# Counting pass of the routing graph's edge ranking: from layer 1's feed-forward to layer 0's, its table kept in DRAM in between

## The chip, the cores and the metric

The kernel is one program on one core of one Trainium2 chip. The metric is the device time of one execution in microseconds (us). Every time below is of this one core.

## What is computed

The reference is a graph transformer of four layers over 3125 nodes of 256 features. Each layer adds a message-passing step over 50,000 edges and a token mixer, then a feed-forward step. Cut to what this change touches:

```python
x = x + L0_gnn(xn, ...) + L0_mix(xn)
x = x + L0_ffn(layernorm(x))        # 8 experts of width 1024, one expert per node, capacity 489
xn = layernorm(x)
x = x + L1_gnn(xn, ...) + L1_mix(xn)
x = x + L1_ffn(layernorm(x))        # one router for all nodes: two of 8 experts, width 512, then a layer norm
...
x = x + L3_ffn(layernorm(x), L3_ffn_edge_index)   # a graph attention picks the experts
```

The last step has a graph of its own, `L3_ffn_edge_index`: 32,768 edges among 2048 nodes, in no order. Its attention is summed by destination node. The kernel therefore sorts these edges by destination long before layer 3: for each edge it computes its place in the sorted list. That depends on the input `L3_ffn_edge_index` alone, so it can be done at any time before the edges are moved, in layer 2's feed-forward.

## The kernel before, in words

The 3125 nodes are padded to 25 tiles of 128 nodes. The 32,768 routing edges stand in 256 chunks of 128 (one column of a 128 x 256 array each); a destination is split into its low seven bits (`ka`, the row in a tile) and its tile (`kt`, 0 to 15, `T2` = 16).

`route_places` (L2039) finds the places in three passes, and gives control back (`yield`) after each group of four chunks, so that a caller can mix it with other work:

- The counting pass. For each group, VectorE compares the low bits of 4 x 128 edges with a row of numbers (`within`, `r_oha`, L2073), and once in 32 chunks the tiles (`tiles`, `r_oht`, L2067). TensorE multiplies the two one-hot arrays, four bf16 products of 16 columns (`count`, L2081): how many edges of the chunk go to each node. ScalarE copies 32 chunks' counts into the table `r_by` (L2083).
- The scan. VectorE sums the table over all chunks (`deg2`, L2096), TensorE turns the sums into starting places (`starts`, L769 and L771), and for each of 16 tiles VectorE runs a prefix sum over the chunks and splits the result in two bytes, `hi` and `lo`, both kept in `r_by` (128 partitions x 2 x 16 x 256 values in bf16, that is 16 KB a partition, L2104 to L2109).
- The ranking pass. For each group, SyncE loads the edges' low bits as a row repeated on all partitions (`r_b`, from the DRAM array `rowa`, L2132); VectorE makes one comparison of it (`r_at`, L2135) and four masked ones (`r_m`, L2138); TensorE runs eight small products (`rank`, L2118 and L2119). After each 16 chunks VectorE picks the result (`r_sel`, `r_pos`, L2122 and L2125).

All three passes lie beside layer 1's feed-forward: `beside(self.l1_ffn(p, after1), (low, 3, 1))` in `fast` (L2621) takes three steps of `route_places` for each step of `l1_ffn` (L1542). Before its loop, `l1_ffn` computes the router from the mean of all nodes (`L1557` and the lines after it), and GpSimd gathers the two chosen experts' weights by index (L1582). Then it runs over seven blocks, six of four node tiles and one of a single tile: for each of two experts, matrix products into `hT` (L117 is the helper that issues them), ScalarE's Gelu, products back, and VectorE's additions into `z` (L1606). At the end of a block comes a layer norm on VectorE (L157 to L165, L1629 to L1631) and the next layer's norm and transposes (`after1`: `norm_tiles`, L182 to L193, transposes on TensorE L173), then the products for layer 2's table (`fill2`).

Layer 0's feed-forward, `l0_ffn` (L1186), runs alone before, as `for _ in self.l0_ffn(p, True, pr0)`. It computes each node's slot in its expert's list on VectorE (L1214 to L1231; `wi`, L1229, is the list of slots), GpSimd scatters 25 tiles of nodes into a DRAM buffer by those slots (`moe_buf`, L372), and for eight experts SyncE loads weights and slots (`xb`, L1248), TensorE transposes (L1253), one half of `xT` is copied by VectorE and one by ScalarE (L125 and L127), and the products run (L117), with VectorE adding the bias (`y`, L1265).

Beside both feed-forward steps a `Pump` releases one scatter of another sort (`by_src`, L372, on GpSimd) for every 700 columns of products in layer 0's step and every 560 in layer 1's; layer 2 starts with a load of the table that these fill.

The engines run their own instruction lists in order and wait for each other by semaphores. The order within each list is fixed when the program is built: GpSimd's is the order of the program text, the others' is set by a scheduler with a cost model of its own. So a generator that is placed beside another says how far ahead it may run, and the built program says in which order the instructions stand.

Of the kernel before, what the change touches and what calls it, by code (L numbers as in the profile page):

```python
# [7 lines left out]
F32 = mybir.dt.float32  # L8
# [75 lines left out]
def beside(main, *others):  # L84

    for i, _ in enumerate(main):
        for g, num, den in others:
            for _ in range((i + 1) * num // den - i * num // den):
                next(g, None)
# [11 lines left out]
class Net:  # L101
# [1934 lines left out]
                nc.scalar.copy(rec[:, :, k], self.load(tmp, n, a[n], dtype=I32))  # L2036
        return rec, place

    def route_places(self, pool, place):  # L2039

        nc = self.nc
        G = 4
        n, per = C2, 32
        dst = self.load(pool, "r_dst", self.a["dst2"], dtype=I32)
        ka = self.bits(pool, dst, "r_a", None, 127)  # L2050
        kt = self.bits(pool, dst, "r_t", 7)
        by = pool.tile([P, 2, T2, n], BF16, name="r_by")
        hi, lo = by[:, 0], by[:, 1]
        pos = pool.tile([P, n], F32, name="r_pos")
        rowa = self.dram.tile([1, n * P], BF16, name="rowa")
        rows_a = rowa.rearrange("o (c p) -> (o c) p", p=P)
        for c0 in range(0, n, P):
            p = self.ps(P)
            nc.tensor.transpose(p, ka[:, c0:c0 + P], self.ident)
            ra = pool.tile([P, P], BF16, name="r_ra", bufs=2)  # L2060
            nc.vector.tensor_copy(ra, p)
            nc.sync.dma_start(rows_a[c0:c0 + P], ra)
        ioa = self.iota2[:, None, :P].to_broadcast([P, G, P])

        def tiles(c0, w):
            oh = pool.tile([P, per, T2], BF16, name="r_oht", bufs=2)[:, :w]
            nc.vector.tensor_tensor(oh, self.iota2[:, None, :T2].to_broadcast([P, w, T2]),  # L2067
                                    kt[:, c0:c0 + w, None].to_broadcast([P, w, T2]), op=OP.is_equal)
            return oh

        def within(g):
            oh = pool.tile([P, G, P], BF16, name="r_oha", bufs=4)
            nc.vector.tensor_tensor(oh, ioa, ka[:, g * G:(g + 1) * G, None].to_broadcast([P, G, P]), op=OP.is_equal)  # L2073
            return oh

        late = []

        def count(g, oha, oht, p, c0):
            for j in range(G):
                k = g * G + j - c0  # L2080
                nc.tensor.matmul(p[:, k * T2:(k + 1) * T2], oha[:, j, :], oht[:, k, :], start=True, stop=True)  # L2081
            if (g + 1) * G == c0 + 32:
                nc.scalar.copy(lo[:, :, c0:c0 + 32], p.rearrange("p (c t) -> p t c", t=T2))  # L2083

        for c0 in range(0, n, per):
            oht = tiles(c0, per)
            p = self.ps(per * T2, name="acc")
            for g in range(c0 // G, (c0 + per) // G):
                late.append((g, within(g), oht, p, c0))
                if len(late) > 2:  # L2090
                    count(*late.pop(0))
                yield
        while late:
            count(*late.pop(0))
        nc.vector.memset(self.deg2, 0.0)
        nc.vector.tensor_reduce(self.deg2[:, :T2], lo, axis=AX.X, op=OP.add)  # L2096
        base = self.starts(pool, self.deg2[:, :T2], T2)
        one = pool.tile([P, n], BF16, name="r_one")
        nc.vector.memset(one, 1.0)
        for t in range(T2):  # L2100
            w = pool.tile([P, n], F32, name="r_w", bufs=2)
            wi = pool.tile([P, n], I32, name="r_wi", bufs=2)
            wl = pool.tile([P, n], I32, name="r_wl", bufs=2)
            nc.vector.memset(w[:, 0:1], 0.0)  # L2104
            nc.vector.tensor_tensor_scan(w[:, 1:], one[:, 1:], lo[:, t, :n - 1], 0.0, OP.mult, OP.add)
            nc.vector.tensor_scalar(wi, w, base[:, t:t + 1], None, op0=OP.add)
            nc.vector.tensor_scalar(wl, wi, 255, None, op0=OP.bitwise_and)
            nc.vector.tensor_copy(lo[:, t, :], wl)
            nc.vector.tensor_sub(hi[:, t, :], wi, wl)  # L2109
            yield  # L2110
        per //= 2

        def rank(g, at, m, oht, q, c0):
            for j in range(G):
                c = g * G + j
                k = c - c0
                v = q[:, k * 2 * T2:(k + 1) * 2 * T2]
                nc.tensor.matmul(v, at[:, j, :], by[:, :, :, c], start=True, stop=False)  # L2118
                nc.tensor.matmul(v[:, T2:], m[:, j, :], oht[:, k, :], start=False, stop=True)  # L2119
            if (g + 1) * G == c0 + per:  # L2120
                sel = pool.tile([P, per, 2 * T2], F32, name="r_sel", bufs=2)
                nc.vector.tensor_tensor(sel.rearrange("p c (b t) -> p c b t", b=2),  # L2122
                                        q.rearrange("p (c b t) -> p c b t", b=2, t=T2),
                                        oht[:, :, None, :].to_broadcast([P, per, 2, T2]), op=OP.mult)
                nc.vector.tensor_reduce(pos[:, c0:c0 + per], sel, axis=AX.X, op=OP.add)  # L2125

        for c0 in range(0, n, per):
            oht = tiles(c0, per)
            q = self.ps(per * 2 * T2, name="acc")
            for g in range(c0 // G, (c0 + per) // G):  # L2130
                b = pool.tile([P, G, P], BF16, name="r_b", bufs=4)
                nc.sync.dma_start(b.rearrange("p g e -> p (g e)"), bcast_rows(rowa[:, g * G * P:(g + 1) * G * P], G * P))  # L2132
                at = pool.tile([P, G, P], BF16, name="r_at", bufs=4)
                m = pool.tile([P, G, P], BF16, name="r_m", bufs=4)
                nc.vector.tensor_scalar(at, b, self.iop, None, op0=OP.is_equal)  # L2135
                for j in range(G):
                    c = g * G + j
                    nc.vector.scalar_tensor_tensor(m[:, j, :], b[:, j, :], ka[:, c:c + 1], self.triu16,  # L2138
                                                   op0=OP.is_equal, op1=OP.mult)
                late.append((g, at, m, oht, q, c0))  # L2140
                if len(late) > 2:
                    rank(*late.pop(0))
                yield
        while late:
            rank(*late.pop(0))
        self.rows_of(pool, pos, n, place)

        nc.vector.tensor_scalar(kt, kt, T2 - 0.5, 65536.0, op0=OP.is_gt, op1=OP.mult)
        nc.vector.tensor_add(place, place, kt)
        nc.vector.tensor_reduce(self.beyond, kt, axis=AX.X, op=OP.add)  # L2150
# [390 lines left out]
    def fast(self):  # L2541
# [3 lines left out]
        with tc.tile_pool(name="keepf", bufs=1) as keep, tc.tile_pool(name="dramf", bufs=1, space=DRAM) as dram:  # L2545
# [30 lines left out]
            with Banks(self, **plain):  # L2576
                sorted_e = dram.tile([P * C1, 3], F32, name="by_src")
                send = self.send(sorted_e, place, rec, C1)
                for _ in range(16):
                    next(send)  # L2580
                with tp("ffn0") as p:
                    self.pump = Pump(tc, send, 700)
                    for _ in self.l0_ffn(p, True, pr0):
                        pass


            with tp("att1") as gp:
# [17 lines left out]
            with Banks(self, **plain):  # L2605
                route = tp("route")
                rec4, place4 = self.route_lists(route.__enter__())
                by_dst = dram.tile([P * C2, 2], F32, name="by_dst")
                nc.sync.dma_start(by_dst.rearrange("(p c) f -> p (c f)", p=P).rearrange("p (k f) -> p k f", k=2),
                                  self.zeros[:, None, :].to_broadcast([P, 2, D]))  # L2610
                self.dlin2 = dram.tile([1, lin_size(C2)], F32, name="dlin2")
                send4 = self.send(by_dst, place4, rec4, C2)
                with tp("set2") as sp, tp("low") as lp, tp("ffn1") as p:
                    tab, fill2 = self.linear_table("tab2", sp, self.load(sp, "w", wtile(a["L2_gnn_W"])))

                    def after1(t0, n):
                        self.norm_tiles(t0, n)
                        fill2(t0, n)
                    self.pump = Pump(tc, send, 560)
                    low = self.route_places(lp, place4)  # L2620
                    beside(self.l1_ffn(p, after1), (low, 3, 1))  # L2621
                    self.pump = None
                    for _ in low:
                        pass
                for _ in send:
                    pass
# [322 lines left out]
```

## Time and profile before

| | |
|---|---|
| median of 3 runs | 4421.31 us (4421.1 to 4431.99) |
| profiled execution: its own time / its span | 4425.03 us / 4423.3 us |
| mean granted TensorE clock in it | 0.851 |
| TensorE products busy | 3472.8 us, 79% |
| VectorE busy | 2187.9 us, 49% |
| ScalarE busy | 913.9 us, 21% |
| GpSimd busy | 2620.9 us, 59% |
| layer 0's feed-forward, products of the experts | about 726 to 952 us |
| layer 1's feed-forward, from the router's product to the last table row | about 1679 to 2085 us |

In the profile's lines PE is TensorE's products, PEld its weight loads, DVE VectorE, ACT ScalarE, POOL GpSimd and SP SyncE. A line of the timeline gives start, duration, engine, line of the kernel, operation, output and inputs, their shapes and the number of instructions merged; the bracket at its end is the idle time of the engine just before, and what ended it. A line of the chain of waits gives start and length of one piece of the chain of work that ended last. A line of the table of windows gives, for each engine, its busy time in that stretch and the number of instructions, then the granted TensorE clock, the share of the DMA engines' time and the rate.

### The profile page before, as it was taken

The numbers are of one execution on the slowest core, as the hardware profiler recorded it, in microseconds if no ns is written. First come the engines' busy times: TensorE is split into PE (matmuls) and PEld (weight loads), VectorE is DVE, ScalarE is ACT, GpSimd is POOL, SyncE is SP. The second block draws the span as 40 slices with busy tenths as digits, with TensorE's granted clock in tenths as the row PEclk, the third lists the DMA queues.
The fourth block names the chain that finished last, engine by engine and source line by source line (L and its number), as shares of the span: only waits on it lengthen the run. The fifth ranks groups of instructions, "written<-read, shape, count | busy, mean of one in ns | idle before, by whom it ended". The sixth has DMA issues, their size and how long they took to land.

```text
span 4423.3 us, 45241 instructions
## 1 busy us (share of the span) xinstructions
PE 3472.8 (79%) x12927; PEld 2207.6 (50%) x12927; DVE 2187.9 (49%) x7489; ACT 913.9 (21%) x1841; POOL 2620.9 (59%) x2609
## 2 busy tenths in 40 slices
PE   8778875963866776686887758996969899669999
PEld 3446543642433443454555434553546577346666
DVE  4576531125777777676445452111255723354554
ACT  2110001210211112112311021221213233132433
POOL 0577776774777765664777734674027656617661
PEclk9888876986877876787988968997979999769999
DMA  3433333323533331022333320000023433421110
GB/s 142 154 98 98 101 97 121 112 59 97 158 101 96 106 92 44 10 51 56 109 106 121 119 88 1 14 10 13 29 74 108 129 93 98 127 61 15 20 15 13
DMA packets 231337, 349.00 MB, mean 79 GB/s; under 512 B 74144, under 2 KB 168151, under 8 KB 231080
## 3 DMA queue, kind: packets, MB, share of 16 engines
q0 software_dynamic: 108384, 219.50, 18.2%
q1 hardware_dynamic: 118280, 122.48, 8.9%
q10 hardware_dynamic: 4416, 4.01, 0.3%
q8 instruction: 110, 1.80, 0.2%
q14 instruction: 147, 1.20, 0.1%
HBM read 295.13 MB, written 50.61 MB: 78 GB/s over the span
## 4 chain that ended last, share of the span: by engine, by line
PE 59%; DVE 15%; DMA 13%; issue 7%; POOL 3%; ACT 2%; SPq 0%; POOLq 0%; DVEq 0%; ACTq 0%
PE mm L117 37%; PE seg L461 10%; DMA G<-tab,e3src 4%; PE seg L445 4%; DMA G<-h_tab,gi 3%; DMA ring<-l1rows,e1src 1%; DMA G<-tab,e1src 1%; PE mm L173 1%; DVE E L457 1%; POOL G L496 1%; DVE ring L912 1%; DVE ln_st L182 1%; DVE r_m L2138 1%; PE mm L1427 1%; PE ga L868 1%
## 5 line engine op out<-in xcount | busy, mean ns | idle before, releaser
L461 PE MATMUL seg<-G,E 128*128 128x257 f32 (+1 forms) x1564 | 503.9, 446 | 144.0 <-DMA G<-h_tab,gi 72.3
L117 PE MATMUL mm<-xnT,w 128*128 128x512 f32 (+1 forms) x1232 | 543.1, 580 | 4.8 <-DVE x L2319 4.5
L496 POOL DMA_INDIRECT G<-h_tab,gi x391 | 384.1, 982 | 257.3 <-DMA rb_L_gnn_self_b<-in_L_gnn_self_b 122.7
L372 POOL DMA_INDIRECT by_src<-rec,place x391 | 418.2, 1070 | 189.3 <-PE mm L117 123.2
L900 POOL DMA_INDIRECT ring<-l1rows,e1src x391 | 438.8, 1122 | 119.9 <-issue 63.1
L457 DVE TENSOR_SCALAR E<-iota_row,e1dl 128x128 f32<-128x128 f32 x1173 | 334.0, 299 | 321.0 <-PE seg L461 305.3
L496 POOL DMA_INDIRECT G<-tab,e1src x391 | 384.1, 982 | 182.5 <-PE seg L461 109.8
L461 PEld LDWEIGHTS seg<-G,E 128*128 128x128 f32 x1564 | 301.0, 213 | 328.5 <-DVE E L457 112.1
L496 POOL DMA_INDIRECT G<-tab,e3src x391 | 387.7, 992 | 123.4 <-PE seg L445 60.0
L461 PE MATMUL seg<-ring,E 128*128 128x264 f32 (+1 forms) x1294 | 366.7, 396 | 93.5 <-DVE E L457 66.0
L445 PE MATMUL seg<-G,E 128*128 128x256 f32 x1070 | 328.3, 433 | 112.8 <-DMA G<-tab,e3src 84.4
L117 PE MATMUL mm<-w,hT 128*128 128x256 f32 (+1 forms) x1712 | 415.0, 389 | 0.7 <-ACT hT L1619 0.5
L372 POOL DMA_INDIRECT by_dst<-rec,place x256 | 252.0, 984 | 193.9 <-PE mm L117 148.9
L461 PEld LDWEIGHTS seg<-ring,E 128*128 128x128 f32 x1294 | 238.6, 213 | 237.2 <-DVE E L457 134.0
L117 PEld LDWEIGHTS mm<-w,hT 128*128 128x128 f32 (+1 forms) x1712 | 313.8, 191 | 54.2 <-issue 14.3
L900 POOL DMA_INDIRECT ring<-l3rows,e2src x256 | 243.7, 952 | 133.4 <-PE mm L117 74.5
L117 PEld LDWEIGHTS mm<-xnT,w 128*128 128x128 f32 x1232 | 224.9, 201 | 190.2 <-issue 176.5
L445 PEld LDWEIGHTS seg<-G,E 128*128 128x128 f32 x1070 | 204.1, 209 | 225.7 <-DMA G<-tab,e3src 71.8
L433 DVE TENSOR_SCALAR E<-iota_row,e3dl,rec 128x128 f32<-128x128 f32 (+1 forms) x391 | 144.1, 382 | 221.9 <-PE seg L445 220.1
L173 PE MATMUL mm<-ident,xn 128*128 128x128 f32 x400 | 93.2, 390 | 177.9 <-DVE xn L193 133.5
L1782 DVE SCALAR_TENSOR_TENSOR x<-mm,l2t_r,x 128x256 f32<-128x256 f32 x150 | 70.8, 482 | 290.5 <-PE mm L117 290.4
L912 DVE TENSOR_TENSOR ring<-ring,ex 128x260 f32<-128x260 f32 (+1 forms) x647 | 188.9, 320 | 2.8 <-ACT ex L891 2.3
(738 smaller groups left out, 5330.4 us busy)
## 6 DMA issues: line engine op xcount, KB each, us to landing
w<-in_L_ffn_w SPq DMA_DIRECT2D x16, 1024.0 KB
h_tab<-htab_s SPq DMA_DIRECT2D x25, 512.0 KB
r_b<-rowa SPq DMA_DIRECT2D x64, 128.0 KB
bn_h<-c_h SPq DMA_DIRECT2D x50, 128.0 KB
G<-h_tab,gi POOLq DMA_INDIRECT x391
by_src<-rec,place POOLq DMA_INDIRECT x391
ring<-l1rows,e1src POOLq DMA_INDIRECT x391
G<-tab,e3src POOLq DMA_INDIRECT x391
```

What stands on the lines that cost most here:

```text
L117: m = self.nc.tensor.matmul(out, l, r, start=(i == 0), stop=(i == last))
L173: self.nc.tensor.transpose(p[:, i * P:(i + 1) * P], src(t0 + i)[:, k * P:(k + 1) * P], self.ident)
L182: nc.vector.bn_stats(st[:, t, :], self.x[:, t, :])
L372: return self.nc.gpsimd.indirect_dma_start(out=table, out_offset=bass.IndirectOffsetOnAxis(ap=idx, axis=0), in_=src, in_offset=None, bound ...
L433: self.nc.vector.tensor_scalar(e[:, :w], self.iota2[:, :w], g["dl"][:, c:c + 1], weight[:, c:c + 1], op0=OP.is_equal, op1=OP.mult)
L445: self.nc.tensor.matmul(A[t], e, rows_c, start=first, stop=last)
L457: nc.vector.tensor_scalar(e, self.iota_row, g["dl"][:, c:c + 1], None, op0=OP.is_equal)
L461: self.product = nc.tensor.matmul(A["sum"], e, rows_c, start=(c == 0 or window(c - 1, nt) != k), stop=last).ins
L496: nc.gpsimd.indirect_dma_start(out=ring[i % len(ring)][:, :D], out_offset=None, in_=table, in_offset=bass.IndirectOffsetOnAxis(ap=gidx[:, ...
L900: got = nc.gpsimd.indirect_dma_start(out=ring[:, i % size].rearrange("p h f -> p (h f)"), out_offset=None, in_=table, in_offset=bass.Indir ...
L912: nc.vector.tensor_mul(r[:, :, :d + 1], r[:, :, :d + 1], EX[c // CB][:, c % CB, :, None].to_broadcast([P, 4, d + 1]))
L1782: nc.vector.scalar_tensor_tensor(self.x[:, t, :], p, r[:, t, e:e + 1], self.x[:, t, :], op0=OP.mult, op1=OP.add)
```

## The change

`route_places` is cut in two. The keys and the one-hot of tiles become `route_keys`, which both halves call. `route_counts` holds the counting pass and the scan, and writes the finished table of 2 MB to a DRAM array `bytab`. `route_places` keeps the ranking pass; it loads the keys again and the table from `bytab`. `route_counts` is run beside layer 0's feed-forward, one step for each of its steps, from a pool `cnt4` that is opened ahead of that step's own pool. In layer 1's feed-forward four steps of the ranking are taken ahead, and then three for every two steps of `l1_ffn`. The counting pass has two `r_oha` buffers in place of four, and one scan buffer of each kind in place of two.

```diff
-    def route_places(self, pool, place):
+    def route_keys(self, pool):
+        nc = self.nc
+        dst = self.load(pool, "r_dst", self.a["dst2"], dtype=I32)
+        ka = self.bits(pool, dst, "r_a", None, 127)
+        kt = pool.tile([P, C2], F32, name="r_t")
+        nc.vector.tensor_scalar(dst, dst, 7, None, op0=OP.logical_shift_right)
+        nc.vector.tensor_copy(kt, dst)
+
+        def tiles(c0, w):
+            oh = pool.tile([P, w, T2], BF16, name="r_oht", bufs=2)
+            nc.vector.tensor_tensor(oh, self.iota2[:, None, :T2].to_broadcast([P, w, T2]),
+                                    kt[:, c0:c0 + w, None].to_broadcast([P, w, T2]), op=OP.is_equal)
+            return oh
+        return ka, kt, tiles
+
+    def route_counts(self, pool):
         nc = self.nc
         G = 4
         n, per = C2, 32
-        dst = self.load(pool, "r_dst", self.a["dst2"], dtype=I32)
-        ka = self.bits(pool, dst, "r_a", None, 127)
-        kt = self.bits(pool, dst, "r_t", 7)
+        ka, kt, tiles = self.route_keys(pool)
         by = pool.tile([P, 2, T2, n], BF16, name="r_by")
         hi, lo = by[:, 0], by[:, 1]
-        pos = pool.tile([P, n], F32, name="r_pos")
-        rowa = self.dram.tile([1, n * P], BF16, name="rowa")
+        self.rowa = rowa = self.dram.tile([1, n * P], BF16, name="rowa")
+        self.bytab = self.dram.tile([P, 2 * T2 * n], BF16, name="bytab")
...
-            oh = pool.tile([P, G, P], BF16, name="r_oha", bufs=4)
+            oh = pool.tile([P, G, P], BF16, name="r_oha", bufs=2)
...
-                if len(late) > 2:
+                if len(late) > 1:
                     count(*late.pop(0))
...
-            w = pool.tile([P, n], F32, name="r_w", bufs=2)
-            wi = pool.tile([P, n], I32, name="r_wi", bufs=2)
-            wl = pool.tile([P, n], I32, name="r_wl", bufs=2)
+            w = pool.tile([P, n], F32, name="r_w")
+            wi = pool.tile([P, n], I32, name="r_wi")
+            wl = pool.tile([P, n], I32, name="r_wl")
...
-        per //= 2
+        nc.sync.dma_start(self.bytab, by.rearrange("p b t c -> p (b t c)"))
+
+    def route_places(self, pool, place):
+        nc = self.nc
+        G = 4
+        n, per = C2, 16
+        ka, kt, tiles = self.route_keys(pool)
+        by = pool.tile([P, 2, T2, n], BF16, name="r_by")
+        nc.sync.dma_start(by.rearrange("p b t c -> p (b t c)"), self.bytab)
+        pos = pool.tile([P, n], F32, name="r_pos")
+        rowa = self.rowa
+        late = []
...
-                with tp("ffn0") as p:
+                with tp("cnt4") as cp, tp("ffn0") as p:
                     self.pump = Pump(tc, send, 700)
-                    for _ in self.l0_ffn(p, True, pr0):
-                        pass
+                    beside(self.l0_ffn(p, True, pr0), (self.route_counts(cp), 1, 1))
...
                     low = self.route_places(lp, place4)
-                    beside(self.l1_ffn(p, after1), (low, 3, 1))
+                    for _ in range(4):
+                        next(low)
+                    beside(self.l1_ffn(p, after1), (low, 3, 2))
```

More of the change, by code (lines that the diff above doesn't have):

```diff
@@ L2063, in route_places @@
         ioa = self.iota2[:, None, :P].to_broadcast([P, G, P])
[L2065 to L2069, printed above, removed]
         def within(g):
-            oh = pool.tile([P, G, P], BF16, name="r_oha", bufs=4)
+            oh = pool.tile([P, G, P], BF16, name="r_oha", bufs=2)
             nc.vector.tensor_tensor(oh, ioa, ka[:, g * G:(g + 1) * G, None].to_broadcast([P, G, P]), op=OP.is_equal)
```

## The prediction

> **What bounds the kernel now.** I read the chain of waits first, then the table of windows for both feed-forward steps, then the timeline around single lines. In layer 1's feed-forward the chain goes through VectorE's norms, then one transpose (L173) per block, then the next block's products. The starts of these transposes give the block periods:
>
> ```profile
> 1754.08 1.77 PE mm L173 x7
> ...
> 1804.30 1.56 PE mm L173 x6
> ...
> 1871.29 2.19 PE mm L173 x8
> ...
> 1935.16 1.97 PE mm L173 x8
> ...
> 1999.80 1.97 PE mm L173 x8
> ...
> 2064.21 2.19 PE mm L173 x8
> ```
>
> The differences are 50.2 (with counting), 67.0 (deg and scan), and 63.9, 64.6, 64.4 us (with ranking). The windows show why:
>
> ```profile
> 684.00:722.00 38.00, 0.11 (x1) 0.00 (x0) 3.43 (x12) 0.00 (x0) 24.66 (x25) 0.50 0.24 86
> 726.00:952.00 226.00, 222.77 (x812) 148.00 (x813) 30.77 (x100) 47.31 (x72) 169.42 (x172) 0.99 0.30 91
> ...
> 1872.00:2064.00 192.00, 146.41 (x871) 96.85 (x870) 159.18 (x508) 29.64 (x45) 113.52 (x98) 0.81 0.20 48
> ```
>
> In the ranking blocks (last row) VectorE is busy 159.18 of 192 us; PE, which has the work, 146.41. VectorE's ranking stands in the norms' way, and that is path. Layer 0's experts (second row) are the opposite: PE 222.77 of 226, VectorE 30.77. Before them (first row) PE is empty for 38 us, because GpSimd scatters nodes:
>
> ```profile
> 687.67 1.00 POOL L372 DMA_INDIRECT moe_buf<-xn,wi  x1 [13.24 <-DVE slot L1230]
> ```
>
> The 25 scatters come 1.29 us apart from 687.67 on and start when VectorE's slot list `wi` is there. Whatever stands ahead of `wi` on VectorE moves them all.
>
> **What the Trainium skill says.** "TensorE: Matmul & The Clock Gate", section "Wait — 56ns, not 53.3ns?": small products start no closer than about 25 ns. The trace agrees: eight counting products took 0.21 us, 26 ns each (1786.48 to 1786.69). "Perfetto Trace Analysis", section "Tensor Engine Instruction": VectorE, ScalarE and GpSimd run strictly in order, PE pulls only weight loads ahead. Agrees: PE stood 5.30 us for the sum of the table. "DMA: Bandwidth & Descriptors", section "Queues, rings and completion order": a sequencer's transfers are taken from its rings in order, so a load waits behind the 4 MB of weights ahead of it. Its section "Bandwidth" gives 341 GB/s at 1 MB; the trace has 281 between 668 and 684.
>
> **The change, part by part.** The order of instructions in the built programs tells what stands where; all times are from the trace of before.
>
> *Layer 0, ahead of `wi`.* One `r_oht` of 256 (0.34) and five `r_oha` (0.61 each, their pitch in layer 1) now stand before `wi` on VectorE, with two small conversions: about 0.4 + 6 x 0.61 = 4.1 us, and the scatters, `xb` and the experts go with it. `r_a` before them lies beside PE's router work: 0. Its load `r_dst` stands behind the first expert's 2.2 MB on SP's queue; at 281 GB/s and issued near 670 it lands near 677, needed at 682; late it would cost up to 2.
>
> *Layer 0, PE empty.* Of the 256 counting products (64 groups of four), 128 lie ahead of or among the first expert's transposes. VectorE needs 32 x 0.61 = 20 us for them and has 38: 0. The other half lies in and between experts: 40 products in gaps after transposes (0) and 88 among products, in fours: at 26 ns 2.3, I take 3. ScalarE's 8 copies and SP's two `rowa` stores lie beside it (ScalarE is busy 47 of 226): 0; if a copy came before a Gelu on the path it would be 0.6.
>
> *Layer 0, the table.* The sum over the table (4.4 us on VectorE) is followed by `starts` on PE, and in the order built, products of the sixth expert stand behind `starts`. Before, this stall was:
>
> ```profile
> 1836.84 4.40 DVE L2096 TENSOR_REDUCE deg<-r_by 128x16 f32<-128x4096 bf16 x1
> ...
> 1841.29 0.61 PE L769 MATMUL mm<-deg,triu 128*128 128x16 f32 x2 [5.30 <-DVE deg L2096]
> ```
>
> I take 5.3 again; 3 if the scheduler's order has slack, 8 if VectorE is late. Then 16 scan steps of 1.75 us, 28 us on VectorE, stand among the last experts' `y` and `xT`, which have 28.46 us each (27.2 of products): VectorE's own 4 us per expert fit between, I take 2 (0 to 5). Transposes and the rest 0.5. The 2 MB store, about 7 us at 281 GB/s, starts behind the last expert's weights and lies beside two experts' products: 0, or 3 if the end of the step had to wait for it. Sum: 4.1 + 3 + 5.3 + 2 + 0.5 = **15 us more** (8 to 23).
>
> *Layer 1, ahead of the blocks.* The table's load (2 MB) and `r_dst` again stand on SP's queue ahead of four `r_b`, then the router's operands. 2.77 MB at about 0.3 MB per us from 1671.5 put `r_b` at 1681.5; four groups of `r_at` and `r_m` (about 5.4 us) then stand ahead of the router's weighting L1557 (1679.68 before), which comes near 1687, 7.3 later. In before, 14.3 us of VectorE's work lay between it and the list for the gathers, of which 4.4 was routing that is now gone; so the gathers (1694.37) and all blocks start **3.1 us later** (0 to 8).
>
> *Layer 1, the blocks.* Before, each step of `l1_ffn` took three groups, with 8 steps a block; now one and a half, 12 groups a block. In block 1 of before, 34.6 us lie between the transposes (1754.08) and the last addition into `z` (1788.70), then 15.6 us to the next transposes, of which 11 `r_oha` and one `r_oht` took 7.3. Without them the tail is 8.3; the same subtraction at 2050.39 to 2064.21 gives 8.5. I take 8.4. In the new order a tail holds 11 `r_m` (0.265), 3 `r_at` (0.27), an `r_oht` and an `r_sel` with `r_pos` (1.2): 5.3. The last addition stands behind seven `r_m` and `r_at`: 2. An `r_m` behind the norm: 1. PE has 12 groups of 8 small products at 42 ns, a third of them in idle places: 1.3 in the block. Period 34.6 + 1.3 + 2 + 8.4 + 5.3 + 1 = **52.6**. A check the other way: 24 groups made 64.2 out of about 44, 0.84 a group; 12 make 54. Unlike before, no deg and scan block is left.
>
> Block 0 ends its products at 1754.08 + 3.1 + 0.6 = 1757.8; three periods of 52.6 give 1915.6; block 4, with two thirds of the ranking, 47.5 (1963.1); block 5, bare, 34.6 + 8.4 + 1 = 44 (2007.1); the last tile 20.9 as before: 2028.0. Before it was 2085.1: **57 us less** (40 to 75).
>
> GpSimd's `by_src` scatters in this step, 192 of 1.29 = 248 us, start at 1712 plus 3 and could end at 1963, ahead of 2028: not the bound, 65 us of cover.
>
> *Sum.* +15 - 57 = **-42 us**. On the profiled execution's 4425.03: 4383. The median of the runs, 4421.31, is 3.7 below that execution; I take the difference off it: **4379**.
>
> **The rivals.**
> 1. *Layer 1 comes out better.* The scheduler hides the ranking in VectorE's idle 9 us per block: period 48, 4.6 x 4 = 18 less, and layer 0 costs 9 instead of 15. For it: block 1 of before had twice the groups at 50.2. Against: the tail's instructions stand there in the built order. 4421 - 75 + 9 = **4355**.
> 2. *The new waits take part of it.* The 2 MB load stands ahead of the router's operands: prologue +12 in place of +3.1; scans stand ahead of `y` and `xT`: +10 in place of +2. For it: both stand in order in front of path work. -42 + 17 = -25: **4396**.
> 3. *No difference.* The end of layer 1 is set by GpSimd's scatters, which the load of their table in layer 2 waits for. For it: they ran until 2050.3 in before. Against: the 65 us above; they are released by columns of products, and those come earlier. **4421**.
> 4. *Slower.* One mechanism: the place of `r_m` and `r_at` in the norms' tails. If what makes a ranking block 64 us is not the number of groups, but that they stand between the norm's instructions, the period stays and only layer 0's cost remains. Twelve groups fall in about 4.3 blocks' worth, so it is slower from a period of 52.6 + 42 / 4.3 = 62.4; at 66 layer 1 gains nothing: 4421 + 15 = **4436**. Against: VectorE's work per group is unchanged and half as many groups come.
>
> **How the numbers follow.** Main case 0.45 (its own range 4365 to 4393, from the bounds), rival 1 0.22, rival 2 0.20, rival 3 0.06, rival 4 0.07. A measurement of this kernel tells about 0.3%, 13 us, from no change. Faster: the first three, 0.87; same: 0.06; slower: 0.07. A range of 4350 to 4412 takes in the main case and rivals 1 and 2 with their spread, and leaves out the last two, 0.13, and some of the edges.
>
> **What would show it right or wrong.** In the profile after: the first `moe_buf` scatter near 692; expert periods near 28.5 in the first experts; one PE wait of about 5 us ended by deg in the sixth; layer 1's products start near 1726 (15 + 3 later); its transposes 52 to 53 us apart; from router to end about 350 us where it was 406. It is wrong if a ranking block takes 62 or more, if layer 0 grows by over 25, or if VectorE waits for the table's load ahead of the router for over 12.

## The result and the profile after

The changed kernel took 4407.17 us at the median of 6 runs (4401.76 to 4409.4), the kernel before, on the same chip, 4426.65 us (4420.93 to 4435.99): a ratio of 0.9946, 95% interval 0.9931 to 0.9961. In a second batch the same two kernels stood at 4394.77 and 4428.04 us, ratio 0.9930 (0.9912 to 0.9949). So the change saves 20 to 33 us, in the direction and within the range that was predicted, but less than the 42 us of the likeliest case; 4407.17 is 4.8 us from the end of that range, and outside the likeliest case's own, 4365 to 4393. Its profiled execution has a span of 4400.0 us, 23.3 less than before.

The stages, each measured between the same two instructions in both traces:

| stage | before | after | difference |
|---|---|---|---|
| start to layer 0's product L1205 | 682.4 | 676.9 | -5.5 |
| L1205 to the first expert's product | 44.0 | 63.0 | +19.0 |
| the experts, to the product L1281 | 229.7 | 251.1 | +21.4 |
| L1281 to the first addition L1287 | 13.9 | 7.4 | -6.5 |
| on to layer 1's last norm of a full group (L193 at 1665.34 and 1691.56) | 695.3 | 693.1 | -2.2 |
| on to layer 2's first sum (all of layer 1's feed-forward) | 433.1 | 374.3 | -58.8 |
| layer 2's first sum to the end | 2324.9 | 2334.2 | +9.3 |

Layer 1's step gave what was forecast. Its transposes, in the chain of waits of the changed kernel (start, length, line):

```profile
1778.50 1.97 PE mm L173 x8
...
1830.26 1.98 PE mm L173 x8
...
1881.72 1.98 PE mm L173 x8
...
1934.76 1.98 PE mm L173 x8
...
1986.36 2.19 PE mm L173 x8
```

The periods are 51.8, 51.5, 53.0 and 51.6 us, where 50 to 67 stood. The table of windows of the changed kernel, for the stretch ahead of the experts, the experts, and the blocks with ranking, answers to the three rows shown of before:

```profile
685.00:734.00 49.00, 6.83 (x100) 4.55 (x100) 17.59 (x31) 1.75 (x3) 40.53 (x25) 0.50 0.19 67
740.00:991.00 251.00, 236.03 (x958) 156.52 (x958) 91.55 (x255) 48.75 (x75) 182.10 (x180) 0.96 0.30 91
1778.00:1986.00 208.00, 164.84 (x844) 113.08 (x843) 144.09 (x437) 39.52 (x60) 138.81 (x132) 0.85 0.16 38
```

In the last row VectorE is busy 144.09 of 208 us (69%, before 83%). In the first, GpSimd is busy 40.53 us with the same 25 scatters that took 24.66 before. The timelines of GpSimd and VectorE in the changed kernel show which:

```profile
685.24 1.21 POOL L372 DMA_INDIRECT moe_buf<-xn,wi  x1 [16.31 <-DVE wi L1229]
686.75 16.70 POOL L372 DMA_INDIRECT moe_buf<-xn,wi  x1 [0.30 <-issue]
703.76 0.98 POOL L372 DMA_INDIRECT moe_buf<-xn,wi  x1 [0.30 <-issue]
```

```profile
687.46 4.89 DVE L2079 TENSOR_TENSOR r_oha<-iota_row,r_a 128x512 bf16<-128x512 f32 x8
...
698.30 4.29 DVE L2079 TENSOR_TENSOR r_oha<-iota_row,r_a 128x512 bf16<-128x512 f32 x7
```

One scatter lasts 16.70 us, to 703.45. VectorE's unbroken row of comparisons ends at 702.59. The scatter takes its places from SBUF, and each comparison reads two SBUF arrays. The Trainium skill, "SBUF — State Buffer", section "Who interferes with whom", says that a VectorE instruction with two SBUF inputs contends with a GpSimd instruction that reads SBUF. It also tells of a probe in which such instructions stalled no DMA; this trace shows one of 16.70 us beside them. The experiment psum_row tests whether that is the cause here.

The second loss is in the sixth and seventh expert. TensorE's timeline of before has there, for the seventh, a wait of 0.41 us and 13.40 us of products:

```profile
899.08 13.40 PE L117 MATMUL mm<-xT,w 128*128 128x489 f32 x32 [0.41 <-DVE xT L127]
```

In the changed kernel:

```profile
898.20 0.25 PE L2087 MATMUL acc<-r_oht,r_oha 128*128 128x16 bf16 x4
904.05 0.61 PE L769 MATMUL mm<-deg,triu 128*128 128x16 f32 x2 [5.60 <-DVE deg L2102]
904.50 0.59 PE L771 MATMUL mm<-deg,ones 128*128 128x16 f32 x2
904.93 6.99 PE L117 MATMUL mm<-xT,w 128*128 128x489 f32 x12
911.76 13.97 PE L117 MATMUL mm<-w,hT 128*128 128x256 f32 x64
925.57 1.01 PE L1253 MATMUL mm<-ident,xb 128*128 128x128 f32 x8
932.24 3.63 PE L117 MATMUL mm<-xT,w 128*128 128x489 f32 x4 [5.67 <-DVE xT L127]
```

The brackets are two waits: 5.60 us for the sum over the table, 5.67 for the `xT` copy that stood on VectorE behind the scans. After the first, 12 products take 6.99 us.

### The profile page after: what moved, and what is told of

Same layout as the page of the kernel before. It is cut to its first block, busy times and chain, and to the rows that moved or that the text cites. A ratio compares the mean times of both kernels' runs of the same rounds, so it can differ in the third digit from the quotient of the medians.

```text
span 4400.0 us, 45279 instructions
## 1 busy us (share of the span) xinstructions
PE 3495.5 (79%) x12927; PEld 2219.3 (50%) x12927; DVE 2197.2 (50%) x7493; ACT 913.2 (21%) x1841; POOL 2616.1 (59%) x2609
## 4 chain that ended last, share of the span: by engine, by line
PE 60%; DVE 14%; DMA 13%; issue 8%; POOL 3%; ACT 2%; SPq 0%; POOLq 0%; DVEq 0%; ACTq 0%
PE mm L117 38%; PE seg L461 11%; DMA G<-tab,e3src 4%; PE seg L445 4%; DMA G<-h_tab,gi 2%; DMA ring<-l1rows,e1src 2%; DMA G<-tab,e1src 1%; DVE E L457 1%; PE mm L173 1%; POOL G L496 1%; DVE ring L912 1%; DVE ln_st L182 1%; PE ga L868 1%; DVE r_m L2159 1%; PE mm L1427 1%
## 5 line engine op out<-in xcount | busy, mean ns | idle before, releaser
L461 PE MATMUL seg<-G,E 128*128 128x257 f32 (+1 forms) x1564 | 513.2, 453 | 137.3 <-DMA G<-h_tab,gi 62.7
L372 POOL DMA_INDIRECT by_src<-rec,place x391 | 403.8, 1033 | 173.6 <-PE mm L117 96.7
L461 PEld LDWEIGHTS seg<-G,E 128*128 128x128 f32 x1564 | 306.9, 217 | 324.2 <-issue 114.2
L496 POOL DMA_INDIRECT G<-tab,e3src x391 | 388.7, 994 | 123.2 <-PE seg L445 58.8
L461 PE MATMUL seg<-ring,E 128*128 128x264 f32 (+1 forms) x1294 | 369.8, 398 | 94.0 <-DVE E L457 47.9
L445 PE MATMUL seg<-G,E 128*128 128x256 f32 x1070 | 339.5, 445 | 102.6 <-DMA G<-tab,e3src 72.8
L445 PEld LDWEIGHTS seg<-G,E 128*128 128x128 f32 x1070 | 208.7, 214 | 223.6 <-DMA G<-tab,e3src 74.1
```

What stands on the lines that cost most here:

```text
L372: return self.nc.gpsimd.indirect_dma_start(out=table, out_offset=bass.IndirectOffsetOnAxis(ap=idx, axis=0), in_=src, in_offset=None, bound ...
L445: self.nc.tensor.matmul(A[t], e, rows_c, start=first, stop=last)
L461: self.product = nc.tensor.matmul(A["sum"], e, rows_c, start=(c == 0 or window(c - 1, nt) != k), stop=last).ins
L496: nc.gpsimd.indirect_dma_start(out=ring[i % len(ring)][:, :D], out_offset=None, in_=table, in_offset=bass.IndirectOffsetOnAxis(ap=gidx[:, ...
```

## The experiments

Theory after the profile: the cost in layer 0's step is two separate things, GpSimd shut out by the comparisons (16 us), and the sum and scans in TensorE's way (13 to 15 us). Rivals: the long scatter waits for a transfer; the scans' work has no room beside the experts at all; layer 1's gain is smaller than its profile says; the new array in DRAM makes later gathers slower. Columns of the table: L1205 to the first expert's product, the longest `moe_buf` scatter, the experts (first product to L1281), L1281 to the first addition, router's product of layer 1 to layer 2's first sum, all from the profiled execution in us; then the median of the runs and its ratio to the kernel before on the same chip. The row of before has its profile from the first batch and its median from the second. The runs lay on three chips. On the second and third the kernel before itself took 5022 and 5013 us, so times are compared only within a chip.

| kernel (chip) | to first product | longest scatter | experts | to addition | layer 1 | median | ratio (95%) |
|---|---|---|---|---|---|---|---|
| before (1) | 44.0 | 1.0 | 229.7 | 13.9 | 419.7 | 4428.04 | |
| again (1) | 63.0 | 16.7 | 250.5 | 7.8 | 357.2 | 4394.77 | 0.9930 (0.9912 to 0.9949) |
| psum_row (1) | 47.5 | 1.0 | 251.1 | 8.0 | 356.6 | 4385.83 | 0.9905 (0.9888 to 0.9923) |
| spaced_scans (1) | 63.0 | 16.7 | 238.3 | 11.3 | 356.9 | 4394.65 | 0.9921 (0.9902 to 0.9940) |
| layer0_alone (1) | 63.0 | 16.7 | 249.7 | 7.9 | 420.9 | 4463.18 | 1.0082 (1.0063 to 1.0101) |
| psum_spaced (2) | 51.2 | 1.0 | 276.6 | 8.0 | 436.8 | 4984.57 | 0.9912 (0.9880 to 0.9943) |
| psum_spaced_first (2) | 46.0 | 1.3 | 274.0 | 8.1 | 432.2 | 4971.61 | 0.9901 (0.9871 to 0.9932) |
| psum_spaced_first_740 (2) | 46.5 | 1.3 | 266.0 | 6.5 | 441.6 | 4971.48 | 0.9888 (0.9844 to 0.9933) |
| after_products (2) | 45.8 | 1.0 | 297.1 | 6.1 | 432.8 | 4987.22 | 0.9931 (0.9907 to 0.9955) |
| again_2 (3) | 63.5 | 16.7 | 287.6 | 8.0 | 434.0 | 4987.70 | 0.9942 (0.9921 to 0.9963) |
| best_700 (3) | 47.3 | 1.4 | 277.1 | 6.8 | 435.0 | 4967.49 | 0.9914 (0.9887 to 0.9942) |
| best_740 (3) | 47.4 | 1.4 | 265.9 | 5.4 | 437.7 | 4958.66 | 0.9883 (0.9851 to 0.9916) |
| rank_1_1 (3) | 64.3 | 16.7 | 283.3 | 8.0 | 438.9 | 4981.21 | 0.9951 (0.9931 to 0.9971) |

**again**, no edit.

> The changed kernel once more, unaltered, as the yardstick for the other three of this batch. Theory (VectorE's one-hot comparisons shut GpSimd out of the node scatters; scans hold up one expert): about 20 us under the kernel before; one moe_buf scatter of 16 to 17 us where the others take 1.0; 63 us from the product L1205 to the first expert's product; one expert period of 42 to 43 us. The differences that the first profile showed outside the two feed-forward steps (5.5 us earlier into layer 0's step, 2 us less in layer 1's message passing, 9 us more after layer 1's step) are scatter between executions and come out different here. Rival (the new 2 MB array in DRAM makes later gathers slower): the 9 us more after layer 1's step come back with the same sign and size.

The two stages of layer 0 repeat within 0.6 us. The stages outside the two feed-forward steps don't: layer 2's first sum to the end is 1.1 us shorter than before (2323.8), not 9.3 longer, and 2323.8 to 2325.3 in all four kernels of this batch. The rival of the DRAM array falls. Of the 10.7 us between the two profiled executions of the changed kernel, 10.4 lie in this stage, and over half of it in two groups of eight products of TensorE (from 2688.06 and 2708.09 us): they take 6.52 and 6.75 us at a granted clock of 0.55 and 0.53, and 3.70 us each in again, the first of them at 1.00. Why the granted clock differs between executions of one program is not shown. The medians, 33 us here and 20 us in the first batch, rest on runs most of which have no trace.

**psum_row**, the row of numbers of the comparison read from PSUM:

```diff
-        ioa = self.iota2[:, None, :P].to_broadcast([P, G, P])
+        io = self.ps(P, name="io")
+        nc.vector.tensor_copy(io, self.iota_row)
+        ioa = io[:, None, :].to_broadcast([P, G, P])
...
-            with Banks(self, **plain):
+            with Banks(self, mm=5, acc=2, io=1):
```

> The changed kernel, but the row of numbers that the comparisons r_oha are made with is read from PSUM, not SBUF (one of the six mm banks goes to it); the comparison then has one SBUF input and not two. Nothing else moves. Theory: the comparisons no longer shut GpSimd out of SBUF, so no moe_buf scatter takes over 2 us, 47 to 48 us lie between L1205 and the first expert's product (63 in the changed kernel), and the time is 12 to 16 us under the changed kernel (given back in part if a comparison from PSUM is slower, and if GpSimd's backlog of by_src scatters after the experts grows). Rival 1 (the long scatter waits for SP's weight transfers or for a descriptor ring): it stays at 16 to 17 us, time unchanged. Rival 2 (the one fewer PSUM bank holds up the experts): scatters short, but expert periods over 29 us and the time no better.

The scatters and, beside them, the comparisons in this kernel, by GpSimd's and VectorE's timelines:

```profile
691.79 1.00 POOL L372 DMA_INDIRECT moe_buf<-xn,wi  x1 [16.35 <-DVE wi L1229]
693.09 0.99 POOL L372 DMA_INDIRECT moe_buf<-xn,wi  x1 [0.30 <-issue]
694.38 0.99 POOL L372 DMA_INDIRECT moe_buf<-xn,wi  x1 [0.30 <-issue]
```

```profile
694.00 4.86 DVE L2081 TENSOR_TENSOR r_oha<-io,r_a 128x512 bf16<-128x512 f32 x8
```

The same eight comparisons take 4.86 us where they took 4.89, and no scatter takes over 1.0. The place of one input was changed, at the price of a PSUM bank (the experts take 0.1 to 0.7 us more), and 15.5 us of the stage went. So the second SBUF input of the comparisons is the cause; a transfer or a ring is not. That it acts through a shared port is the skill's account; no run here shows the port itself. The comparison `r_oht`, one in nine, keeps both inputs in SBUF in this kernel, and the scatters beside it stay at 1.0 us: a single such instruction did no harm here, the long row did. Of the 15.5 the medians show 9; in the profiled executions, 6.5 us are lost again ahead of L1205 (see the end of the next section).

**spaced_scans**, three empty steps ahead of the starts, and the scans bound to the products:

```diff
+        for _ in range(3):
+            yield
         base = self.starts(pool, self.deg2[:, :T2], T2)
...
-            nc.vector.tensor_tensor_scan(w[:, 1:], one[:, 1:], lo[:, t, :n - 1], 0.0, OP.mult, OP.add)
+            sc = nc.vector.tensor_tensor_scan(w[:, 1:], one[:, 1:], lo[:, t, :n - 1], 0.0, OP.mult, OP.add)
+            self.with_product(sc)
```

Here `with_product` makes an instruction wait for the product that was written last before it.

> The changed kernel, with three empty steps between the sum over the table and its starts on TensorE, and each of the 16 scans bound to follow the product that is latest when it is written. Work is the same. Theory: the two waits of the sixth and seventh experts go (5.6 us for the sum, 5.3 us for the xT copy that stood behind the scans) and with them the slow clock after each (1.8 us twice): the period of 42.7 us falls to 30 or 31, the one after it from 30.2 to under 29, the time by 11 to 14 us. Part may come back as GpSimd's backlog after the experts (up to 5 us). The long scatter stays. Rival (the scans' work itself, 28 us of VectorE, has no room beside these experts): the wait moves to another y or xT, gain under 4 us.

TensorE's timeline of this kernel at the same place:

```profile
905.30 5.17 PE L117 MATMUL mm<-xT,w 128*128 128x489 f32 x12
911.05 0.40 PE L769 MATMUL mm<-deg,triu 128*128 128x16 f32 x2 [0.58 <-DVE deg L2106]
911.29 0.38 PE L771 MATMUL mm<-deg,ones 128*128 128x16 f32 x2
911.52 14.06 PE L117 MATMUL mm<-w,hT 128*128 128x256 f32 x64
925.41 1.01 PE L1253 MATMUL mm<-ident,xb 128*128 128x128 f32 x8
927.86 13.40 PE L117 MATMUL mm<-xT,w 128*128 128x489 f32 x32 [1.44 <-DVE xT L127]
```

The waits of 5.60 and 5.67 us are 0.58 and 1.44, and the 12 products that took 6.99 us after the stall take 5.17: the stall itself was 5 us, the slower products after it another 1.8. The experts are 12.2 us shorter than in again. The rival, that the scans have no room, falls. But the wait behind the experts grew by 3.5 us, and the medians of the two kernels are equal. In the stage the gain is shown; in the total it is not. (The profile of this kernel, too, has 6.5 us more ahead of L1205 than that of again.)

**layer0_alone**, the kernel before with the counting of the change beside layer 0's step, its table unused:

```diff
-                with tp("ffn0") as p:
+                with tp("cnt4") as cp, tp("ffn0") as p:
                     self.pump = Pump(tc, send, 700)
-                    for _ in self.l0_ffn(p, True, pr0):
-                        pass
+                    beside(self.l0_ffn(p, True, pr0), (self.route_counts(cp), 1, 1))
```

> The kernel before, with the change's counting run beside layer 0's feed-forward in addition, its table unused; layer 1's feed-forward counts, scans and ranks as before. So this is the cost side of the change alone. Theory: layer 0's step gets 40 us longer (19 ahead of the experts, 21 in them), 6 of it come back from GpSimd's shorter backlog: 30 to 38 us slower than the kernel before, that is 4452 to 4460. By the prediction's sum it would be 15 us slower, 4436. Rival (the gain of layer 1's step was smaller than its profile says, and layer 0's cost is nearer 20): under 4445.

35 us slower at the median, as the theory has it, not the prediction's 15. Layer 1's step is as long as before (420.9), so the cost and the gain of the change are separate, and the gain is the difference: 4463.18 less 4394.77 is 68 us by medians. By the profiles it is 60.0 when counted from layer 1's last norm of a full group, as in the table of stages, and 63.7 by the column of layer 1, which begins at the router's product and so leaves out what the change adds ahead of it.

**psum_spaced**, both edits, psum_row's and spaced_scans', in one kernel.

> Both earlier edits in one kernel: the comparisons' row in PSUM, and the scans spaced out. If the two costs are separate, both go: 47.5 us from L1205 to the first expert's product, 238 to 239 us from there to the product L1281, no scatter over 2 us. Against the changed kernel that is 28 us in layer 0's step; GpSimd's backlog of by_src scatters after it grows back from 8 to 13 us or more, so 18 to 24 us under the changed kernel, 4370 to 4380. Rival (the backlog is the next bound: all of what the experts gain beyond 15 us is waited for behind by_src): fin to the first addition 18 us or more, and no faster than with the PSUM row alone.

**psum_spaced_first**, and the comparisons bound to come behind the slot lists, with `self.behind(i, self.slots)` in `within` and `tiles` (`self.slots` is the instruction of `ri`, L1231).

> The kernel psum_spaced, with the one-hot comparisons bound to come after the slot lists wi and ri on VectorE. Expected: the first scatter 5.2 to 5.6 us after L1205 (8.3 in the changed kernel, 5.2 in the kernel before), 44 to 45 us to the first expert's product, all else as psum_spaced: 3 us less at most, some of it lost to the backlog. Rival: counting that begins 3 us later reaches into the experts, and their periods grow by as much.

**psum_spaced_first_740**, and `Pump(tc, send, 740)` in place of 700 beside layer 0's step.

> The kernel psum_spaced_first, with one by_src scatter for every 740 columns of products beside layer 0's experts in place of 700, so that some ten fewer lie there and that many more in layer 1's step. Theory (layer 0's step ends with a wait for the scatters that are behind): fin to the first addition falls by 8 us or more, to the 5 to 6 us that one gather takes, and layer 1's step keeps its length, as its scatters ended 20 us ahead of its last block: 6 to 10 us under psum_spaced_first. Rival (layer 1's step or layer 2's load of by_src waits for what was moved): fin shorter, but layer 1's step longer by the same.

**after_products**, the changed kernel with only its comparisons bound to the products (`self.with_product` around the comparison in `within`).

> The changed kernel, with each comparison r_oha (row in SBUF as in the change) bound to follow the product that is latest when it is written, so that none runs before the first expert's products. A second way to clear the scatters of VectorE's two-input work. Theory: 44 to 45 us from L1205 to the first expert's product (63 in the changed kernel), no long scatter; all 64 groups now stand among the products, so the first five experts take 30 to 31 us each, and L1205 to L1281 comes to 303 us (314 in the changed kernel, 273.7 before). Rival (the long scatter came from something else that starts there): it stays.

These four ran on the second chip, and absolute expectations can't be held against it. What carries over: the long scatter is gone in all four, also in after_products, where the comparisons keep their two SBUF inputs and only their time differs. The group of its scatters, by tile, gives shortest, median and longest in ns:

```profile
L372 POOL DMA_INDIRECT moe_buf<-xn,wi x25: 983/984/997, 775.9 to 806.8; - x25
```

The slot lists come 2.8 us earlier once the comparisons stand behind them (first scatter 6.0 us after L1205, 8.8 in psum_spaced). after_products has its counting among the products, takes 297.1 us for the experts (the other three 266.0 to 276.6), and has the highest ratio of the four, though the intervals overlap. The backlog of 12 us or more was not seen: 2 to 4 `by_src` scatters were left when the experts ended, where before on the first chip had 8 and spaced_scans 6. Nor is it shown that the two edits together save more than the first alone: the ratio is 0.9912 for psum_spaced and 0.9905 for psum_row on the first chip.

**again_2**, **best_700** and **best_740** repeat the changed kernel, psum_spaced_first and psum_spaced_first_740 side by side.

> The changed kernel unaltered, as the yardstick of this batch on its chip. On a chip like the first: 20 to 33 us under the kernel before, with 63 us from L1205 to the first expert's product and 250 to 251 us from there to L1281.

> The kernel psum_spaced_first again, beside the changed kernel on one chip, since the batch before ran on another chip, on which the kernel before took 5022 us. On a chip like the first: 44 to 45 us from L1205 to the first expert's product, 238 to 239 us from there to L1281, fin to the first addition 12 to 15 us (GpSimd's backlog), and 18 to 26 us under the changed kernel. Rival (the backlog takes it all): under 10.

> The kernel psum_spaced_first_740 again on this chip: as best_700, but fin to the first addition 5 to 7 us, layer 1's step as long as in the changed kernel (357 us), so 5 to 9 us under best_700. Rival: layer 1's step longer by what was moved, no difference to best_700.

They ran on the third chip. best_700 is 20 us under the changed kernel by medians, but the intervals overlap; best_740 is 29 us under it, 0.9883 (0.9851 to 0.9916) against 0.9942 (0.9921 to 0.9963), which do not. best_740 thus beats both kernels. The fewer scatters made the wait after the experts 1.4 us shorter (1.6 on the second chip), not 8. In both pairs of profiles the kernel with 740 has shorter experts, by 11.2 us on the third chip and 7.9 on the second, and a longer step of layer 1, by 2.8 and 9.3 us, so the recorded rival, that layer 1's step pays for what was moved there, does not fall. Between best_700 and best_740 the intervals overlap, and whether 740 is better than 700 stays open.

**rank_1_1**, one ranking group for each step of layer 1's feed-forward:

```diff
-                    beside(self.l1_ffn(p, after1), (low, 3, 2))
+                    beside(self.l1_ffn(p, after1), (low, 1, 1))
```

> The changed kernel, with one ranking group for each step of layer 1's feed-forward in place of three for two: 8 groups in each of the six blocks in place of 12 in five, and 10 left over after the last block. Theory (a block's period is the bare 44 us and then about 0.65 us for each group, wherever it stands): all six periods near 49.5 (now 51.5 to 53 in four, 51.2, 44.3), and 8 to 14 us more after the last block; 3 to 9 us slower in all. Rival (what lengthens a block is the place of a few groups in the norm, not their number): periods stay at 51 to 53 in all six, 15 us slower or more.

Inconclusive. On this chip the changed kernel's blocks with 12 groups take 65.0 to 67.3 us, its block with 9 groups 64.3 and its bare block 51.8; with 7 or 8 groups the periods are 62.2 to 64.6, where a straight line gives 61 for 8. The total is the same.

## Why the prediction was right in sign and range, and its gain too large

- **Ahead of `wi`**: forecast +4.1. The first scatter came 8.3 us after L1205, before 5.2: +3.1. Near; `r_dst` was there in time (its first reader on VectorE, at 676.76, did not wait).
- **"Layer 0, PE empty ... VectorE needs 32 x 0.61 = 20 us for them and has 38: 0."** This step failed. VectorE did have the time, but the stretch belongs to GpSimd, and the comparisons held up one of its scatters: the 25 took 47.9 us in place of 32.0, +15.9 (in psum_row 32.0 again). The prediction looked for cover on VectorE and TensorE, not on the engine that everything waited for. The trace of before had the warning, in layer 1's step, where `by_src` scatters run beside the counting:

```profile
1744.96 6.16 POOL L372 DMA_INDIRECT by_src<-rec,place  x1 [0.30 <-issue]
```

```profile
1744.37 0.68 DVE L2073 TENSOR_TENSOR r_oha<-iota_row,r_a 128x512 bf16<-128x512 f32 x1
1744.97 1.21 DVE L1629 TENSOR_TENSOR z<-z,rb_L_ffn_gamma 128x1024 f32<-128x1024 f32 x1
...
1749.58 0.68 DVE L2073 TENSOR_TENSOR r_oha<-iota_row,r_a 128x512 bf16<-128x512 f32 x1
```

  Twice there, at 1744.96 and 1795.18, a scatter takes 6.16 us beside an unbroken row of VectorE instructions with two SBUF inputs (comparisons, and the norm's products with gamma, additions of beta and of `z`). Both end 0.86 us after the row's end, and so does the one of 16.70 us.
- **Counting among products**: forecast 3.5 with the transposes. The first expert grew by 0.7, the fourth and fifth by 2.3 and 2.5, and about 1.6 of the sixth's growth is not its waits: 7. The mis-sized term is the price of a group among the products, about 0.1 us in the prediction:

```profile
863.73 1.89 PE L117 MATMUL mm<-xT,w 128*128 128x489 f32 x4
865.46 0.25 PE L2087 MATMUL acc<-r_oht,r_oha 128*128 128x16 bf16 x4
865.56 1.89 PE L117 MATMUL mm<-xT,w 128*128 128x489 f32 x4
```

  Four products with a group take 1.83 us from start to start, without one 1.66 (an eighth of the 13.24 us from the first of 32 to the next row of products): about 0.18 a group, 4.0 for the 22 groups. Another 0.7 us goes, in the fourth and fifth period each, between the transposes and the next expert's first product (2.10 from start to start, before 1.41), where eight counting products and VectorE's comparisons stand around the `xT` copy, and 0.9 to the four products of `starts`.
- **The sum**: forecast 5.3, found 5.6, and 1.8 that was not in the working: the products after the stall are slower (12 in 6.99 us, 5.17 without it). The Trainium skill, "TensorE: Matmul & The Clock Gate", section "Part 1: The HAM clock gate (the "warmup" mystery)", tells of a half clock after an idle window; the trace agrees: after the wait for `xT`, four products took 3.63 us at a granted clock of 0.50, elsewhere 1.89 at 1.00.
- **The scans**: forecast 2 (0 to 5), found 5.3 for the `xT` copy behind them, and 1.8 again (32 products in 15.20 us, 13.40 before).
- **After the experts**, not in the working: -6.5. In the kernel before, GpSimd still had 10 us of `by_src` scatters to do when the experts ended, and the gathers of the result stood behind them in its order:

```profile
965.86 0.98 POOL L372 DMA_INDIRECT by_src<-rec,place  x1 [0.30 <-issue]
967.15 0.99 POOL L366 DMA_INDIRECT yt<-moe_y,ri  x1 [0.30 <-issue]
```

  Eight such scatters were left there; with longer experts, three were left in the changed kernel:

```profile
994.33 0.98 POOL L372 DMA_INDIRECT by_src<-rec,place  x1 [0.30 <-issue]
995.62 0.98 POOL L366 DMA_INDIRECT yt<-moe_y,ri  x1 [0.30 <-issue]
```

  In the changed kernel the first gather starts 4.6 us after L1281 (991.05), before 11.0 (956.15 to 967.15).
- **Layer 1's step**: forecast -57 with its prologue, found -58.8. The three ranking blocks were given 52.6 and took 51.8, 51.5 and 53.0, the bare one 44 and took 44.4. In the sum of 52.6 one term does not fit its words: 96 small products at 42 ns are 4.0 us, and with a third of them in idle places 2.7 remain, not 1.3. The terms were not measured one by one, so the good total does not show that each of them is right. Block 4 was given 47.5 for fewer groups and took 51.6; between its transposes stand 9 groups, 12 in each of the three others. Fewer groups did not make its period shorter, so their number alone does not set it; rank_1_1 points the same way, and what does set it stays open. The prologue was given +3.1 and took +0.7 to the first gather (29.7 us after the norm, before 29.0), and nothing to the first product. The router's weighting L1557 came 5.8 us later (20.1 us after that norm, before 14.3; forecast 7.3), behind four groups of ranking on VectorE. Their first `r_b`, issued at 1699.73, 2.3 us behind the table's 2 MB, was used at 1706.41, which fits a load taken in its turn, and VectorE's wait for it was 0.60 us:

```profile
1706.41 0.35 DVE L2156 TENSOR_SCALAR r_at<-r_b,iop 128x512 bf16<-128x512 bf16 x1 [0.60 <-DMA r_b<-rowa]
```

Together: 19.0 + 21.4 - 6.5 - 58.8 = -24.9 in the two steps, where 15 - 57 = -42 was forecast. Layer 0's step grew by 33.9 where 15 stood (40.4 until L1281, less the 6.5), layer 1's shrank by 1.8 more than forecast. The prediction had named growth of layer 0 by over 25 as a sign that it is wrong: by that sign its account of layer 0 failed, and the time lies within the range in part because the range had room for the rivals, and because 6.5 us came back that stood in no part of the working. That part is luck. Rival 2 had nearly the measured time (4396), but only half by its own mechanism: the scans did hold up `xT`, the table's load did not hold up the gathers. Rivals 3 and 4 fall: layer 1's step got shorter, and its periods did not stay at 64.

What stays open: the stretch up to L1205 takes 677 us in the changed kernel (both times) and in layer0_alone, and 682 to 684 in the kernel before, psum_row and spaced_scans. spaced_scans has there the same instructions in the same order on TensorE and VectorE as the changed kernel. What differs is the granted clock, the third number from the end in these rows of the table of windows, first of the changed kernel, then of spaced_scans:

```profile
420.00:435.00 15.00, 14.13 (x70) 11.53 (x68) 12.67 (x46) 0.96 (x2) 9.96 (x11) 0.89 0.30 86
420.00:435.00 15.00, 15.00 (x59) 12.41 (x60) 9.63 (x35) 0.96 (x2) 8.23 (x9) 0.66 0.25 70
```

It is 1.00 there in again and layer0_alone, 0.67 in before and 0.66 in psum_row. The same products of TensorE fall 3.3 us behind in this stretch in spaced_scans and 1.7 more between 441 and 446 us, 5.0 of the 6.6 us. Why the clock differs there stays open: with one profile for most kernels it can't be told whether it goes with the kernel or with the execution. It hides gains of this size in the totals.

## What to carry to other kernels

Work that is put where TensorE is idle is free only if the engine that TensorE waits for is not slowed: name that engine first, and ask what it shares with the work that comes. On VectorE, a long row of instructions with two SBUF inputs beside GpSimd's indirect transfers is such a case, and moving one small input to PSUM settled it here. A trace of before can show the price in another place: look for single transfers there that take far longer than their like. A wait that a moved step brings along costs more than its length when the products after it run slowly, so give it other products to stand behind (here that shortened the stage by 12.2 us, and the total not measurably).

## What the runs showed of the hardware that was not expected

A single indirect transfer of GpSimd, 1.0 us by itself, lasted 16.7 us, until 0.86 us after the end of a row of VectorE comparisons with two SBUF inputs; it didn't get in between two of them. This was so in six profiles of four kernels whose comparisons stood there with both inputs in SBUF (16.7 each time), on both chips where such a kernel ran, and in none of the six with one input in PSUM (1.4 at most), nor in after_products, where the comparisons stand elsewhere (1.0). Beside the shorter rows of before it was 6.16 us, twice.

The same program took 4428 us on one chip and 5013 to 5022 on two others, with a mean granted TensorE clock of 0.85 on the first and 0.81 on the others. Why is not shown. The ratio of the change was the same: 0.9930 to 0.9946 on the first, 0.9942 on the third.
